# Twenty narrow scans for the rows of nodes in a graph layer, with their limits counted ahead of a branch

## The chip, the cores and the metric

The kernel runs on one core of a Trainium2 chip. The metric is the device time of one launch in microseconds: 3378.7 us is the median of three runs before the change (3378.27 to 3379.26). The profile is one execution on the same core, with a span of 3379.6 us.

## What is computed

One layer of a graph network over 10000 nodes with 512 features and 160000 edges, sorted by destination. The layer adds three things to `x`: a message sum over edges, a linear attention, and a mixture of experts whose weights are set once, from the mean of all rows.

```python
xn = _layernorm(x, axis=-1)
# message sum
h = jnp.matmul(xn, W)
msgs = h[edge_src] * edge_weight[:, None]
agg = jax.ops.segment_sum(msgs, edge_dst, num_segments=X.shape[0])
gnn = jax.nn.relu(agg + bias)
# linear attention, 8 heads of 64
q = jax.nn.softmax(q, axis=-1) * scale
k = jax.nn.softmax(k, axis=-2)
context = jnp.einsum('bhnd,bhne->bhde', k, v)
out = jnp.einsum('bhde,bhnd->bhne', context, q)
# x = x + gnn + gamma_layer_norm(out @ w_out); then x = x + experts(_layernorm(x))
dst = jnp.minimum((10000 * jax.random.uniform(..., (160000,)) ** 2.0).astype(jnp.int32), 9999)
```

The last line matters here. The destinations are 10000 times the square of a uniform number, so about 160000 times the root of node/10000 edges come before those of a node: low nodes have many edges, high ones few.

## The kernel before

**Chunks.** The nodes are worked in twenty chunks of 512 (the last has 272), each as four sub-rows of up to 128 partitions: partition p and sub-row s hold node base + 4p + s.

**Key stage.** For each chunk TensorE turns the normalised rows (`pt`, L197), multiplies them with the key and query weights (`pk`, `pq`, L205), and adds up `ek` times rows (`pc`, L779). ScalarE takes exponentials. VectorE adds the keys' sums (`kacc`, L766), makes the softmax of the queries from PSUM (`qs`, `qt`, L188 to L190), copies turned rows out of PSUM (L199) and adds `pc` to `G` (L782). The program order of TensorE is written out by hand (`manual_schedule`); the other engines' order is made by a scheduler that places each instruction by its inputs and by its estimate of when engines come free.

**Edges.** The 160000 edges are 1250 tiles of 128. GpSimd fetches the 128 source rows of a tile with one indirect transfer (`msg`, L485) into one of 24 slots. Tiles are joined to windows: the first 896 tiles in pairs, the other 354 alone, so there are 802 windows (`NW`; `PAIRED` is 448). `bases` holds the first destination of each window, the same in all partitions. For each tile VectorE builds a selection matrix `sel` (L492, L494) that places an edge's weight in one of 32 rows, row = destination minus the window's base. TensorE multiplies `sel` with `msg` (`pm`, L503), ScalarE copies the sum, and it is stored to `part_d`, 32 rows to a window. A node that two windows share is put right later (`carry`, L557 to L579). In the key stage a planner (`work`) places edge products in TensorE's order, one tile for each 0.93 us of planned work.

**Finding rows.** To add a node's sum, the kernel must know its row in `part_d`. Row = node + sum over all windows whose base is at most the node of `jump`, where `jump` is 32 minus the gap to the base before. `find_rows` (L443) does this for a chunk: four scans over all 802 windows (L449), each a `scalar_tensor_tensor` that compares `bases` with the nodes, multiplies with `jump` and adds up along the row; then two small steps (L454, L455) turn the four sums into row numbers `row_of`. It is called for five chunks when the edges are placed, and for the other fifteen at the end of their own chunk in the key stage; there `behind` keeps the scans after the last `G` addition. The intermediate `past` and the `gap` of `place_edges` share one buffer (tag `past`).

**The branch.** The shortcuts hold only for edges that are spread evenly enough. So `place_edges` counts the conditions that hold in the columns of `count`: two sums over tiles and windows, and one comparison for each of ten limits `AT_HAND` (L439). `oddities` adds the columns (L537), lets TensorE add the partitions (L539), and compares with `ALL_GOOD`, the count when all hold. After the key stage every engine loads the result and branches (L614, L615): if any condition fails, a general path runs. The page's profile is of a run that skips it.

**After the branch.** TensorE turns `G` (needs VectorE), makes the context and then works chunk by chunk on attention (`po`) and on the graph product (`pg`), with edge products in between. GpSimd gathers node sums by `row_of` (`at`, L865) between the `msg` gathers. When all edges are done the expert stage runs, with TensorE alone as its pace.

Of the kernel before, what the change touches and what calls it, by code (L numbers as in the profile page):

```python
# [9 lines left out]
F32 = mybir.dt.float32  # L10
I32 = mybir.dt.int32
AF = mybir.ActivationFunctionType
ALU = mybir.AluOpType
# [3 lines left out]

P = 128
SQ = 32
SUB = 4  # L20
EPS = 1e-5
HEAD = 64
QSCALE = HEAD ** -0.5
PAIRED = 448
GROUP = 4
WIN = P // GROUP
# [6 lines left out]
AT_HAND = [(5, 320), (7, 384), (9, 448), (11, 512), (13, 576), (14, 640), (15, 672), (16, 704), (17, 736), (18, 756)]  # L33
# [13 lines left out]
def gps_layer_kernel(  # L47
# [19 lines left out]
    nc = tc.nc  # L67
    N, D = x.shape
    NET = src.shape[1]
# [10 lines left out]
    chunks = []  # L80
    base = 0
    while base < N:
        rows = min(P, (N - base) // SUB)
        chunks.append((base, rows))
        base += rows * SUB
    assert base == N
    NCH = len(chunks)

    def tokens(t, c):
        b, r = chunks[c]  # L90
        return t[b : b + r * SUB, :].rearrange("(p s) d -> p s d", s=SUB)

# [6 lines left out]
    make_identity(nc, ident)  # L99
    half_neg = const.tile([P, SUB], F32, name="half_neg")  # L100
    nc.gpsimd.memset(half_neg, -0.5)
# [13 lines left out]
    for last in sorted({b - a for a, b in zip(CARRIES, CARRIES[1:])}):  # L115
# [3 lines left out]
                                fill=0.0, base=1 - last, channel_multiplier=1)  # L119
    node = const.tile([P, NCH, SUB], F32, name="node")  # L120
    nc.gpsimd.iota(node, pattern=[[P * SUB, NCH], [1, SUB]], base=0, channel_multiplier=SUB,
                   allow_small_or_imprecise_dtypes=True)
# [19 lines left out]
    NW = NET - PAIRED  # L142
# [9 lines left out]
    def behind(inst, other):  # L152

        tc.add_manual_dep(inst.ins, other.ins.name, mybir.DependencyInfo(
            mybir.DependencyClass.NoSync, mybir.DependencyReason.SCHED_ONLY), reason="order of work")
# [81 lines left out]
    def experts_weights():  # L237
# [12 lines left out]
        for j in range(KB):  # L250
            for g in range(P // SQ):
                nc.gpsimd.dma_start(w1_sb[g * SQ : (g + 1) * SQ, j, :], features(w1)[j, g, :, : NBASE * P])
        nc.gpsimd.dma_start(w2_sb, w2[: NBASE * P, :].rearrange("(f p) d -> p f d", p=P))
# [4 lines left out]
    def features(t):  # L258

        return t.rearrange("(g j e) h -> j g e h", g=P // SQ, j=KB)  # L260

    def rows_in(c):

        r = chunks[c][1]
        xn = io_f["in"].tile([P, SUB, D], F32, name="xn2")
        if r % SQ:
            for j in range(KB):
                for g in range(P // SQ):
                    nc.sync.dma_start(xn[:r, :, j * P + g * SQ : j * P + (g + 1) * SQ],
                                      x1_d[c][:, :, g * P + j * SQ : g * P + (j + 1) * SQ])  # L270
# [64 lines left out]
    with ExitStack() as ph:  # L335
# [6 lines left out]
        ep = edge_ctx.enter_context(tc.tile_pool(name="edge", bufs=1))  # L342
        ew = edge_ctx.enter_context(tc.tile_pool(name="edge_w", bufs=3))
# [42 lines left out]
        on_w = ep.tile([P, NET], F32, name="on_w")  # L386
        bases = ep.tile([P, NW + 1], F32, name="bases")
        jump = ep.tile([P, NW], F32, name="jump")
        count = ep.tile([P, 2 + len(AT_HAND)], F32, name="count")
        n_big = ep.tile([1, 2], F32, name="n_big")  # L390
        usable = ep.tile([P, 1], F32, name="usable")
        n_odd = ep.tile([1, 1], I32, name="n_odd")
# [1 line left out]
        def place_edges():  # L394
            nc.sync.dma_start(src_sb, src)
            nc.sync.dma_start(w_sb, edge_w)
            dst_sb = tmp.tile([P, NET], I32, name="dst_sb", tag="whole")
            nc.sync.dma_start(dst_sb, dst)
            row_sb = tmp.tile([P, NET], I32, name="row_sb")
            nc.sync.dma_start(row_sb, dst[0:1, :].to_broadcast([P, NET]))  # L400

            nc.vector.memset(bases[:, 0:1], 0.0)
            nc.vector.memset(bases[:, NW:], FAR)
            nc.vector.tensor_copy(bases[:, 1:PAIRED],
                                  row_sb[:, 2 : 2 * PAIRED].rearrange("p (w j) -> p w j", j=2)[:, :, 0])
            nc.vector.tensor_copy(bases[:, PAIRED:NW], row_sb[:, 2 * PAIRED :])
            gap = ew.tile([P, NW], F32, name="gap", tag="past", bufs=1)
            nc.vector.tensor_tensor(gap, bases[:, 1:], bases[:, :NW], ALU.subtract)
            nc.vector.tensor_copy(place, dst_sb)

            def by_window_of(t, per_window, o, op):

                nc.vector.tensor_tensor(
                    o[:, : 2 * PAIRED].rearrange("p (w j) -> p w j", j=2),
                    t[:, : 2 * PAIRED].rearrange("p (w j) -> p w j", j=2),
                    per_window[:, :PAIRED, None].to_broadcast([P, PAIRED, 2]), op)
                nc.vector.tensor_tensor(o[:, 2 * PAIRED :], t[:, 2 * PAIRED :], per_window[:, PAIRED:NW], op)

            by_window_of(place, bases, place, ALU.subtract)

            by_window_of(place, gap, on_w, ALU.is_equal)
            nc.vector.tensor_tensor(on_w, on_w, w_sb, ALU.mult)


            nc.vector.memset(jump[:, 0:1], 1.0)
            nc.vector.tensor_scalar(jump[:, 1:], gap[:, : NW - 1], -1.0, float(WIN), op0=ALU.mult, op1=ALU.add)


            good = tmp.tile([P, NET], F32, name="good", tag="whole")
            by_window_of(place, gap, good, ALU.is_le)  # L430
            nc.vector.scalar_tensor_tensor(good, place, 0.0, good, op0=ALU.is_ge, op1=ALU.mult)
            nc.vector.scalar_tensor_tensor(good, place, float(WIN - 1), good, op0=ALU.is_lt, op1=ALU.mult,
                                           accum_out=count[:, 0:1])
            nc.vector.tensor_scalar(good[:, :NW], gap, 0.0, None, op0=ALU.is_ge)
            nc.vector.scalar_tensor_tensor(good[:, : NW - 1], gap[:, : NW - 1], float(WIN), good[:, : NW - 1],
                                           op0=ALU.is_lt, op1=ALU.mult, accum_out=count[:, 1:2])

            for i, (n, w) in enumerate(AT_HAND):
                nc.vector.tensor_scalar(count[:, 2 + i : 3 + i], bases[:, w : w + 1],  # L439
                                        float(chunks[n][0] if n < NCH else N), None, op0=ALU.is_ge)  # L440

        ALL_GOOD = P * (NET + NW - 1 + len(AT_HAND))

        def find_rows(c, other):

            at = ew.tile([P, SUB], F32, name="at")
            for s in range(SUB):
                past = ew.tile([P, NW], F32, name="past", bufs=1)
                scan = nc.vector.scalar_tensor_tensor(  # L449
                    past, bases[:, :NW], node[:, c, s : s + 1], jump,  # L450
                    op0=ALU.is_le, op1=ALU.mult, accum_out=at[:, s : s + 1])
                if other:
                    behind(scan, other)
            nc.vector.tensor_tensor(at, at, node[:, c], ALU.add)  # L454
            nc.vector.tensor_scalar(row_of[:, c], at, float(ZERO_ROW), None, op0=ALU.min)  # L455

# [77 lines left out]
        def oddities():  # L534
# [5 lines left out]
            n = ew.tile([1, 2], F32, name="n", bufs=1)  # L540
            nc.vector.tensor_scalar(n[:, 0:1], pn, -1.0, float(ALL_GOOD), op0=ALU.mult, op1=ALU.add)
            nc.vector.tensor_scalar(n[:, 1:2], n_big[:, 0:1], -1.0, 1.0, op0=ALU.mult, op1=ALU.add)
# [66 lines left out]
        def general_path():  # L609

            with ExitStack() as pb:
                fp = pb.enter_context(tc.tile_pool(name="far", bufs=1))
                kp = pb.enter_context(tc.tile_pool(name="with_max", bufs=1, side="right"))
                any_odd = nc.values_load(n_odd[0:1, 0:1], min_val=0, max_val=ALL_GOOD + 2)  # L614
                with tc.If(any_odd > 0):  # L615
# [128 lines left out]
        for c, (_, r) in enumerate(chunks):  # L744
            if c == EARLY:
                normal_rows(NCH)
                place_edges()
                next_nodes()
                oddities()
                for soon in range(ROWS_SOON):  # L750
                    find_rows(soon, None)
                norm_ctx.close()
                done[1] = -6 * PACE
                pools["m"] = edge_ctx.enter_context(tc.tile_pool(name="edge_m", bufs=24,
                                                                 reuse_waits="tile"))
                nc.sync.dma_start(wv, w_qkv_t[:, 2 * D :].rearrange("(k p) d -> p k d", p=P))
                nc.sync.dma_start(wo, w_out_t.rearrange("(k p) d -> p k d", p=P))
# [156 lines left out]
        for c, (_, r) in enumerate(chunks):  # L914
            ot, at = ot_next, held["at"]
# [22 lines left out]
            if c == NCH - 1:  # L938
# [3 lines left out]
                                           op0=ALU.mult, op1=ALU.mult)  # L942
            if c < NCH - 1:
                for s in range(SUB):
                    nc.vector.scalar_tensor_tensor(xsum[:r], ot[:r, s, :], mv[:r, s, 1:2], xsum[:r],
                                                   op0=ALU.mult, op1=ALU.add)
# [55 lines left out]
    more = wp.tile([1, 1], F32, name="more")  # L1002
# [242 lines left out]
    with tc.If(any_more > 0):  # L1245
# [9 lines left out]
        for c, (_, r) in enumerate(chunks):  # L1255
# [8 lines left out]
            for f in blocks:  # L1264
                m, at = fsz[f], (f - NBASE) * P
# [55 lines left out]
```

## Time and profile before

| stretch, us | what runs | TensorE busy | VectorE busy | GpSimd busy | granted clock |
|---|---|---|---|---|---|
| 0 to 100 | first loads, rows normalised | 72.2 of 100 | 77.1 | 72.3 | 0.95 |
| 100 to 126 | rows of the first chunks, scans | 20.9 of 26 | 26.0 | 20.8 | 0.96 |
| 150 to 178 | scans, `sel` builds | 24.7 of 28 | 27.1 | 12.4 | 0.89 |
| 400 to 600 | key stage with edges | 200 of 200 | 101.3 | 149.9 | 1.00 |
| 1200 to 1985 | attention, graph product, edges | 753.8 of 785 | 515.4 | 555.5 | 0.99 |
| 2500 to 3000 | experts | 499.6 of 500 | 249.5 | 0 | 1.00 |

Busy is the time in which an engine carries out instructions of its own; a wait for another engine is idle time and is put down to the one that ended it. The granted clock is the share of TensorE's full clock [...]. GpSimd's 0.95 us for a gather is the time to issue it; the data land some microseconds later.

### The profile page before, as it was taken

Reading aid. Unit: us, or ns where it says so; the run is one execution under the profiler, and the core shown is the slowest. Engines: PE = TensorE matmul, PEld = TensorE weight load, DVE = VectorE, ACT = ScalarE, POOL = GpSimd, SP = SyncE. Lnnn points to the kernel's source line nnn. Section 1 sums busy time; section 2 is a strip of 40 time slices with the busy share of each in tenths; the row PEclk is TensorE's granted clock in tenths of the full one; section 3 lists DMA queues with packets and bytes.
Section 4 is the critical chain, followed back from the end, with each engine's and each line's share of the span. In section 5 each row is a group of like instructions: output and inputs, shape, how many; then the busy total and the mean of one; then the engine's idle time right before and its main releaser. Section 6 shows DMA issues by size and latency. Waiting matters only on the chain.

```text
span 3379.6 us, 37367 instructions
## 1 busy us (share of the span) xinstructions
PE 3270.7 (97%) x12969; PEld 1923.8 (57%) x12969; DVE 1842.5 (55%) x4771; ACT 797.3 (24%) x1626; POOL 1433.4 (42%) x1472
## 2 busy tenths in 40 slices
PE   6999999999999899999999999999999999999998
PEld 3444444444443333333333347888888888888886
DVE  7844545455545456666766576544554455445543
ACT  4412121212121121122222123222222222222211
POOL 6667777777777777777777420000000000000000
PEclk9999999999999999999999999999999999999999
DMA  9778888888878888999989751121212121212111
GB/s 363 262 231 254 275 258 279 257 272 263 268 241 262 290 291 304 309 329 325 329 313 329 235 163 50 50 63 50 88 50 63 54 84 50 63 60 78 50 39 40
DMA packets 218332, 644.96 MB, mean 191 GB/s; under 512 B 35486, under 2 KB 75422, under 8 KB 193786
## 3 DMA queue, kind: packets, MB, share of 16 engines
q0 software_dynamic: 108208, 354.02, 33.5%
q1 hardware_dynamic: 67656, 168.51, 15.2%
q10 hardware_dynamic: 42266, 119.91, 9.1%
q8 instruction: 106, 1.74, 0.2%
q14 instruction: 96, 0.79, 0.1%
HBM read 485.32 MB, written 157.00 MB: 190 GB/s over the span
## 4 chain that ended last, share of the span: by engine, by line
PE 54%; DMA 9%; issue 1%; DVE 1%; POOL 1%; ACT 0%; POOLq 0%; DVEq 0%; ACTq 0%; SPq 0%
PE px L1103 15%; PE pz L1103 10%; PE py L1103 10%; PE po L205 7%; DMA msg<-xn_d,src_sb 6%; PE pg L205 6%; PE pm L503 3%; PE ph L1103 2%; PE pt L197 1%; DMA z_d<-xt 1%; POOL msg L485 1%; DMA xt<-x_d 1%; DMA at<-part_d,row_of 1%; DMA x_d<-ot 0%; PE pcarry L568 0%
## 5 line engine op out<-in xcount | busy, mean ns | idle before, releaser
L485 POOL DMA_INDIRECT msg<-xn_d,src_sb x1250 | 1226.5, 981 | 424.8 <-issue 236.6
L503 PE MATMUL pm<-msg,sel 128*32 128x512 f32 x2504 | 356.2, 603 | 28.7 <-DMA msg<-xn_d,src_sb 28.6
L492 DVE TENSOR_SCALAR sel<-iota_w,place,w_sb 128x31 f32<-128x31 f32 x1250 | 305.9, 317 | 103.9 <-PE pm L503 103.7
L205 PE MATMUL po<-G,qT 128*128 128x512 f32 (+1 forms) x640 | 292.7, 604 | 8.0 <-DMA qT<-qT_d 8.0
L205 PE MATMUL pg<-wq,aT 128*128 128x512 f32 (+1 forms) x640 | 293.5, 607 | 5.9 <-ACT aT L199 5.9
L779 PE MATMUL pc<-xn,ek 128*128 128x512 f32 (+1 forms) x640 | 288.7, 601 | 3.7 <-DVE qt L190 3.7
L205 PE MATMUL pk<-wk,xnT 128*128 128x512 f32 (+1 forms) x640 | 285.7, 599 | 0.0
L205 PE MATMUL pq<-wq,xnT 128*128 128x512 f32 (+1 forms) x640 | 284.5, 597 | 0.0
L506 ACT COPY part<-pm 128x512 f32<-128x512 f32 x201 | 118.1, 587 | 629.7 <-PE pm L503 604.7
L503 PEld LDWEIGHTS pm<-msg,sel 128*32 128x32 f32 x2504 | 68.3, 109 | 282.2 <-issue 196.9
L205 PEld LDWEIGHTS pg<-wq,aT 128*128 128x128 f32 (+1 forms) x640 | 116.9, 189 | 182.9 <-issue 162.9
L205 PEld LDWEIGHTS po<-G,qT 128*128 128x128 f32 (+1 forms) x640 | 116.0, 189 | 171.0 <-issue 147.5
L205 PEld LDWEIGHTS pk<-wk,xnT 128*128 128x128 f32 (+1 forms) x640 | 118.1, 188 | 164.4 <-issue 153.1
L205 PEld LDWEIGHTS pq<-wq,xnT 128*128 128x128 f32 (+1 forms) x640 | 117.5, 187 | 165.3 <-issue 159.2
L1103 PE MATMUL px<-xnT,w_sb 128*128 128x256 f32 (+1 forms) x800 | 203.8, 377 | 6.4 <-DVE u L1138 6.3
L779 PEld LDWEIGHTS pc<-xn,ek 128*128 128x128 f32 (+1 forms) x640 | 118.7, 192 | 145.8 <-issue 141.7
L1103 PE MATMUL px<-w_sb,hh 128*128 128x256 f32 (+1 forms) x800 | 185.7, 379 | 0.0
L161 DVE BATCH_NORM_STATS2 st<-ot 128x6 f32<-128x512 f32 (+1 forms) x160 | 110.2, 689 | 138.4 <-ACT ot L903 137.5
L1103 PE MATMUL py<-xs,w_sum 128*128 128x256 f32 (+1 forms) x800 | 185.0, 374 | 0.0
L1103 PE MATMUL py<-w_sum,hh 128*128 128x256 f32 (+1 forms) x800 | 179.2, 379 | 0.0
L1103 PEld LDWEIGHTS px<-xnT,w_sb 128*128 128x128 f32 x800 | 150.3, 191 | 28.5 <-DVE u L1138 8.8
L1103 PEld LDWEIGHTS py<-w_sum,hh 128*128 128x128 f32 (+1 forms) x800 | 150.0, 188 | 22.7
(270 smaller groups left out, 4438.5 us busy)
## 6 DMA issues: line engine op xcount, KB each, us to landing
part_d<-part ACTq DMA_DIRECT2D x201, 256.0 KB
msg<-xn_d,src_sb POOLq DMA_INDIRECT x1250
xn<-in_x SPq DMA_DIRECT2D x19, 1024.0 KB
xn_d<-xn ACTq DMA_DIRECT2D x19, 1024.0 KB
qT_d<-qT ACTq DMA_DIRECT2D x19, 1024.0 KB
qT<-qT_d SPq DMA_DIRECT2D x19, 1024.0 KB
xt<-in_x SPq DMA_DIRECT2D x19, 1024.0 KB
x_d<-ot SPq DMA_DIRECT2D x19, 1024.0 KB
```

Of the source, the lines that this page charges most:

```text
L161: nc.vector.bn_stats(st[:r, s, :], t[:r, s, :])
L197: nc.tensor.transpose(pt[:, s * r : (s + 1) * r], t[:r, s, kb * P : (kb + 1) * P], ident[:r, :r])
L205: nc.tensor.matmul(po[:r, :], t[:, kb, s * r : (s + 1) * r], w[:, kb, :], start=kb == 0, stop=kb == KB - 1)
L485: nc.gpsimd.indirect_dma_start(out=m[k], out_offset=None, in_=xn_d, in_offset=bass.IndirectOffsetOnAxis(ap=src_sb[:, t0 + k : t0 + k + 1], ...
L492: nc.vector.tensor_scalar(sel[:, k, 1:], iota_w, place[:, t0 + k : t0 + k + 1], w_sb[:, t0 + k : t0 + k + 1], op0=ALU.is_equal, op1=ALU.mult)
L503: nc.tensor.matmul(pm[h * WIN : (h + 1) * WIN, :], sel[:, k, :], m[k] if k < len(m) else m[0], start=j == 0, stop=j == batch - 1, skip_gro ...
L506: nc.scalar.copy(part, pm)
L779: nc.tensor.matmul(pc, ek[:r, s, cb * P : (cb + 1) * P], xn[:r, s, :], start=s == 0, stop=s == SUB - 1)
L1103: nc.tensor.matmul(o, lhs[j], rhs[j], start=start and j == 0, stop=stop and j == n - 1, skip_group_check=True)
```

## The change

The destinations' distribution is known, so the windows that can hold a chunk's nodes are too: `window_at` turns a node into a tile number, 1250 times the root of node/10000, and that into a window. `span(c)` gives a range `lo` to `hi` for a chunk, ten tiles (`SPARE`) wider on both sides. The scans then run over windows lo + 1 to hi - 1 alone. What all windows up to `lo` would have added is known without a scan: their `jump` telescopes to 1 + 32 lo - bases[lo]. One more small instruction adds it.

That a range holds depends on the edges at hand, so each range is checked: base `lo` must be at most the chunk's first node, base `hi` at least its end. These forty comparisons go into forty more columns of `count`, and `ALL_GOOD` grows by as much; if one fails, the general path runs as for the other conditions. `gap` gets a buffer of its own.

```diff
+SPARE = 10
...
-        count = ep.tile([P, 2 + len(AT_HAND)], F32, name="count")
+        count = ep.tile([P, 2 + len(AT_HAND) + 2 * NCH], F32, name="count")
...
-            gap = ew.tile([P, NW], F32, name="gap", tag="past", bufs=1)
+            gap = ew.tile([P, NW], F32, name="gap", bufs=1)
...
-
-        ALL_GOOD = P * (NET + NW - 1 + len(AT_HAND))
+            spans_hold()
+
+        ALL_GOOD = P * (NET + NW - 1 + len(AT_HAND) + 2 * NCH)
+        WIDEST = 256
+
+        def window_at(node, more):
+            tile_no = NET * (node / N) ** 0.5 + more
+            return min(max(int(tile_no / 2 if tile_no < 2 * PAIRED else tile_no - PAIRED), 0), NW)
+
+        def span(c):
+            return window_at(chunks[c][0], -SPARE), window_at(chunks[c][0] + SUB * chunks[c][1], SPARE)
+
+        def spans_hold():
+            for c, (b, r) in enumerate(chunks):
+                for i, w, op, edge in ((0, span(c)[0], ALU.is_le, b), (1, span(c)[1], ALU.is_ge, b + SUB * r)):
+                    at = 2 + len(AT_HAND) + 2 * c + i
+                    nc.vector.tensor_scalar(count[:, at : at + 1], bases[:, w : w + 1], float(edge), None, op0=op)
 
         def find_rows(c, other):
 
             at = ew.tile([P, SUB], F32, name="at")
+            lo, hi = span(c)
             for s in range(SUB):
-                past = ew.tile([P, NW], F32, name="past", bufs=1)
+                past = ew.tile([P, WIDEST], F32, name="past_c", bufs=1)[:, : hi - lo - 1]
                 scan = nc.vector.scalar_tensor_tensor(
-                    past, bases[:, :NW], node[:, c, s : s + 1], jump,
+                    past, bases[:, lo + 1 : hi], node[:, c, s : s + 1], jump[:, lo + 1 : hi],
                     op0=ALU.is_le, op1=ALU.mult, accum_out=at[:, s : s + 1])
                 if other:
                     behind(scan, other)
+
+            nc.vector.tensor_scalar(at, at, bases[:, lo : lo + 1], float(1 + lo * WIN), op0=ALU.subtract, op1=ALU.add)
             nc.vector.tensor_tensor(at, at, node[:, c], ALU.add)
```

## The prediction

> **What bounds the kernel now.** First the page's busy times and slices.
>
> ```profile
> PE 3270.7 (97%) x12969; PEld 1923.8 (57%) x12969; DVE 1842.5 (55%) x4771; ACT 797.3 (24%) x1626; POOL 1433.4 (42%) x1472
> PE   6999999999999899999999999999999999999998
> ```
>
> TensorE is busy for 3270.7 of 3379.6 us. All its idle time is 109 us, so an edit of VectorE work is worth only what it takes out of these 109 us, or off whatever else sets the pace in some stretch. Next the groups, for the price of what the change shrinks.
>
> ```profile
> L449 DVE SCALAR_TENSOR_TENSOR past<-bases,node,jump 128x802 f32<-128x802 f32 x80 | 85.0, 1062 | 1.0
> L449 DVE DVE_READ_ACCUMULATOR past<-bases,node,jump 128x1 f32 x80 | 6.5, 82 | 0.0
> ```
>
> Eighty scans of 802 elements, 85.0 us in all: 2.5% of the span, but on an engine that is 55% busy. So the timeline of TensorE must tell where a scan stands before it. Its only idle time between 40 and 1138 us is here (start, length, and in brackets the idle time before it and who ended it):
>
> ```profile
> 116.68 1.47 PE L197 MATMUL pt<-ident,xn 128*128 128x128 f32 x12
> 120.01 0.63 PE L197 MATMUL pt<-ident,xn 128*128 128x128 f32 x4 [1.86 <-DVE minus L366]
> 123.85 8.80 PE L779 MATMUL pc<-xn,ek 128*128 128x512 f32 x16 [3.21 <-DVE qt L190]
> 134.24 7.03 PE L779 MATMUL pc<-xn,ek 128*128 128x512 f32 x16
> ...
> 168.57 1.04 PE L197 MATMUL pt<-ident,xn 128*128 128x128 f32 x8
> 172.00 1.08 PE L197 MATMUL pt<-ident,xn 128*128 128x128 f32 x4 [2.39 <-DVE qt L190]
> 173.56 1.08 PE L197 MATMUL pt<-ident,xn 128*128 128x128 f32 x4 [0.48 <-DVE qt L190]
> 175.12 8.83 PE L779 MATMUL pc<-xn,ek 128*128 128x512 f32 x16 [0.48 <-DVE qt L190]
> ```
>
> Two stalls, both on the softmax rows of L190: VectorE is behind. Around the first it is busy 26.0 of 26 us (100 to 126), around the second 27.1 of 28 (150 to 178). Thirteen of the first twenty scans lie from 88 to 121 us, three from 134 to 142, four from 153 to 159.
>
> A third wait stands at the branch:
>
> ```profile
> 1146.14 3.64 PE L197 MATMUL pt<-ident,G 128*128 128x128 f32 x16 [7.23 <-DVEq L615]
> ```
>
> Last, GpSimd. Its gathers (L485) start every 1.25 us, 0.95 busy and 0.30 between. Up to 985 us some wait for TensorE to free a message slot (8.03 us at 208, 2.07 at 911, 3.08 at 985). After that, to 1903 us, they go back to back with few gaps: 634 gathers and 72 more of L865, 706 x 1.25 = 883 us of a stretch of 914. From 985 on the gathers set the pace. And there some take longer:
>
> ```profile
> 1030.73 0.95 POOL L485 DMA_INDIRECT msg<-xn_d,src_sb  x1 [0.30 <-issue]
> 1031.98 1.74 POOL L485 DMA_INDIRECT msg<-xn_d,src_sb  x1 [0.30 <-DMA msg<-xn_d,src_sb]
> ```
>
> and VectorE's timeline at that place:
>
> ```profile
> 1031.84 1.06 DVE L449 SCALAR_TENSOR_TENSOR past<-bases,node,jump 128x802 f32<-128x802 f32 x1
> ```
>
> The gather that began 0.14 us after a scan took 1.74 us and ended just after it (1033.72, with an add of L766 behind the scan) where its neighbour took 0.95.
>
> [...] sixteen matmuls took 8.80 and 8.83 us after the two stalls, 7.03 elsewhere, and the granted clock from 150 to 178 us was 0.89. [...]
>
> **The change, part by part.**
>
> (1) Shorter scans. From the generated `dst`, the twenty ranges hold 145, 68, 53, 47, 43 windows in the first five chunks and 27 to 60 in the rest, 1066 in place of 16040. Every comparison of a limit holds for them, so the branch stays untaken. [...]
>
> (2) Added: 40 comparisons into `count`, and one `tensor_scalar` for each chunk. Their like are L439 (three in 0.26 us, a step of 0.065) and L455 (0.07). 40 x 0.065 = 2.6 us and 20 x 0.07 = 1.4 us. Bounds for the comparisons: 0.065 as a step, 0.14 as a whole duration (L439's median), so 2.6 to 5.6 us; I take 2.6, since they don't depend on each other.
>
> (3) The order. The scheduler doesn't leave the freed time empty. In the built order the twenty scans of the first five chunks, the comparisons and 22 to 27 `sel` builds (L492; 6 before) now come ahead of the first stall's softmax rows. I added up the VectorE steps from the timeline of before over both orders. Up to the two rows that end the first stall's waits (L190 at 119.18 and 123.03) the sum moves by -0.5 and +0.1 us: the first stall stays. Up to the rows of the next chunk it is 12.4 us less: the `sel` builds that filled 156 to 170 us are done by then. VectorE idled 8.57 us at 141.7 and takes part of them there. So the second stall goes.
>
> What it is worth: from the start of its transposes (168.57) to the next `pc` took 6.55 us, in the undisturbed place (132.49 to 134.24) 1.75; that `pc` took 8.66 in step, undisturbed 6.95. So 4.8 + 1.7 = 6.5 us. TensorE then reaches the first edge product (207.1) 6.5 us earlier. Its messages were gathered from 169.9 to 200.4, and GpSimd waited 8.03 us for that product; 1.5 us of that wait remain. So the gathers, which up to 985 us wait for TensorE, move along, and with them the gather-paced stretch and all that follows.
>
> (4) The three last scan groups (at 1028, 1084 and 1136 us) lie where gathers set the pace. Their four hit gathers took 1.08, 1.74, 1.69 and 1.71 against 0.95: 2.4 us. [...] I take 2.2 us. The scan groups before 985 us also lengthen gathers, by about as much each, but there GpSimd waits for TensorE anyway: nothing.
>
> (5) The branch. VectorE reached it at 1141.6, after the four scans of the last chunk; now `ksum` (TensorE's 1138.9) is last, and it arrives at about 1139.3. TensorE restarts some 2.3 us earlier. But four fewer gathers are queued before the branch (738, not 742), the drain gap at 1150.75 stays, and after it TensorE waits for messages (1161.6). Between 0 and 2.3; alone it gives nothing, since gathers set the pace; with (4) it keeps TensorE out of their way. I take 0.
>
> The 60 scans after 200 us cost TensorE nothing: it is busy 100% from 220 to 1000 us. Nothing after the branch is touched.
>
> Sum: 6.5 + 2.2 = 8.7 us. 3378.7 - 8.7 = 3370.0.
>
> **Rivals.** (a) The gathers, not TensorE, hold the line from their start: xn_d's last write frees them at 169.9, whatever TensorE does. Then the 6.5 us are swallowed and (4) remains: 3376.5. For it: 1326 gathers x 1.25 = 1658 us of 1734. Against it: GpSimd's 39.3 us of waits for `pm` from 180 to 1140.
> (b) The first stall shrinks too, because the small steps are cheaper than I price them. The whole stall is 7.17 - 1.75 + 1.7 = 7.1 us: 3362.9. For it: 13 scans lie there. Against it: the sums over the order.
> (c) Nothing carries: the waits just move to the next DMA. 3378.7. For it: the message waits after 1160.
> (d) Slower: the four gathers put behind the branch meet the weight and row loads that start there (one gather at 1152.12 took 9.46 us to land) and cost their 4 x 1.25 = 5.0 us, while (a) eats the early gain: 3378.7 - 2.2 + 5.0 = 3381.5. The comparisons at 0.14 would add up to 3 us to the first stall.
>
> **How the numbers follow.** Forecast 0.63, (a) 0.13, (b) 0.10, (c) 0.07, (d) 0.07. The forecast's own spread is 3367 to 3372.5 (1 us of drain or branch each way, 2.8 for the comparisons' upper bound, which is partly hidden). The range takes in most of (a) and the near half of (b): 3365 to 3376.6. 0.2% is 6.8 us, 3371.9: faster holds (b) and nine tenths of the forecast, 0.66; same (a), (c) and the rest, 0.27; slower 0.07.
>
> **What would show it.** The scan's group at about 0.2 to 0.3 us mean. The wait of `pt` on `qt` near 172 gone and `pc` at 7.0; the waits near 118 to 124 still there. The first `pm` near 200.6, GpSimd's wait before it 1.5 us. Gathers near 1030, 1088 and 1138 at 0.95 to 1.2. The span to the last gather 8 to 9 us shorter, the last stage as long as before. Wrong if GpSimd shows new waits after the branch, or if the first stall moves by more than 1 us.

## The result, and the profile after

The changed kernel's median was 3365.1 us over four runs, beside 3379.0 for the kernel before: ratio 0.9959, 95% interval 0.9942 to 0.9976, so 8 to 20 us off. Nineteen more runs of the changed kernel, beside 51 of the kernel before, narrow this to 0.9975 (0.9968 to 0.9982): 8.4 us off, between 6.1 and 10.8, median 3369.7. The forecast was 8.7 off, 3370.0. The first four runs had fallen on the good side; how far runs differ is part of what follows.

First the page of the changed kernel, its busy times:

```profile
PE 3262.2 (97%) x12969; PEld 1926.0 (57%) x12969; DVE 1790.6 (53%) x4831; ACT 796.8 (24%) x1626; POOL 1413.5 (42%) x1472
```

VectorE lost 51.9 us, GpSimd 19.9. Then VectorE's groups, the scan, the read of its sum, the extra step and the forty comparisons (count, then busy time and mean ns):

```profile
L467 DVE SCALAR_TENSOR_TENSOR past_c<-bases,node,jump 128x53 f32<-128x53 f32 (+18 forms) x80 | 22.3, 278 | 1.6
L467 DVE DVE_READ_ACCUMULATOR past_c<-bases,node,jump 128x1 f32 x80 | 6.6, 82 | 0.0
L473 DVE TENSOR_SCALAR at<-at,bases 128x4 f32<-128x4 f32 x20 | 4.9, 246 | 0.5
L459 DVE TENSOR_SCALAR count<-bases 128x1 f32<-128x1 f32 x40 | 2.9, 137 | 0.0
```

A scan takes 278 ns in the mean, not 1062. TensorE's timeline at the two stalls and at the branch:

```profile
116.30 1.04 PE L198 MATMUL pt<-ident,xn 128*128 128x128 f32 x8
117.91 0.63 PE L198 MATMUL pt<-ident,xn 128*128 128x128 f32 x4 [0.58 <-DVE qt L191]
120.17 1.09 PE L198 MATMUL pt<-ident,xn 128*128 128x128 f32 x4 [1.63 <-DVE minus L367]
124.47 9.86 PE L799 MATMUL pc<-xn,ek 128*128 128x512 f32 x16 [3.21 <-DVE qt L191]
...
170.25 1.91 PE L198 MATMUL pt<-ident,xn 128*128 128x128 f32 x16
171.99 7.03 PE L799 MATMUL pc<-xn,ek 128*128 128x512 f32 x16
...
202.16 1.92 PE L523 MATMUL pm<-msg,sel 128*32 128x512 f32 x16
...
1138.30 3.65 PE L198 MATMUL pt<-ident,G 128*128 128x128 f32 x16 [4.31 <-DVEq L635]
```

The second stall is gone: sixteen transposes without a wait, `pc` at 7.03. The first one stayed and cost more: `pc` started at 124.47 (before 123.85) and took 9.86 (8.80). The first edge product came at 202.16 instead of 207.08, TensorE's restart after the branch at 1138.30 instead of 1146.14.

How far TensorE is ahead of the kernel before (its lead), in the two profiles of the changed kernel (start of the same product in each trace, subtracted):

| at (time in before) | 116 us | 169 | 187 | 1110 | 1147 | 1200 | 1500 | 1900 | 1930 | end |
|---|---|---|---|---|---|---|---|---|---|---|
| changed | 0.4 | -1.7 | 4.9 | 4.9 | 7.8 | 5.9 | 8.8 | 7.1 | 17.0 | 17.2 |
| changed, again | 1.0 | -0.8 | 5.8 | 5.8 | 8.2 | 7.4 | 6.8 | 8.6 | 8.5 | 8.1 |

Up to the branch the two agree within 1 us. The 9 us between them arise between 1900 and 1930, at the last messages, which the kernel before waited for:

```profile
1912.57 1.88 PE L503 MATMUL pm<-msg,sel 128*32 128x512 f32 x2 [5.03 <-DMA msg<-xn_d,src_sb]
1915.45 1.93 PE L503 MATMUL pm<-msg,sel 128*32 128x512 f32 x6 [0.99 <-DMA msg<-xn_d,src_sb]
1917.31 8.15 PE L205 MATMUL pg<-wq,aT 128*128 128x512 f32 x16
```

and the changed kernel, again, too:

```profile
1904.65 1.88 PE L523 MATMUL pm<-msg,sel 128*32 128x512 f32 x2 [5.68 <-DMA msg<-xn_d,src_sb]
1907.27 1.93 PE L523 MATMUL pm<-msg,sel 128*32 128x512 f32 x6 [0.73 <-DMA msg<-xn_d,src_sb]
1909.13 7.86 PE L206 MATMUL pg<-wq,aT 128*128 128x512 f32 x16
```

In the first profile of the changed kernel no wait stood there, and the sixteen products after it took 7.13 us. Over all profiles on chips of this speed the wait was 0 to 10.7 us, in no relation to the edit: none in the changed kernel and two others, 10.7 with narrow scans in the last three chunks. So it is a landing that differs from run to run, for a cause that no run shows.

### The profile page after: what moved, and what is told of

Its sections match the earlier page's. It is cut to its first block, busy times and chain, and to the rows that moved or that the text cites. A ratio compares the mean times of both kernels' runs of the same rounds, so it can differ in the third digit from the quotient of the medians.

```text
span 3362.2 us, 37437 instructions
## 1 busy us (share of the span) xinstructions
PE 3262.2 (97%) x12969; PEld 1926.0 (57%) x12969; DVE 1790.6 (53%) x4831; ACT 796.8 (24%) x1626; POOL 1413.5 (42%) x1472
## 3 DMA queue, kind: packets, MB, share of 16 engines
q8 instruction: 106, 1.74, 0.2%
## 5 line engine op out<-in xcount | busy, mean ns | idle before, releaser
L505 POOL DMA_INDIRECT msg<-xn_d,src_sb x1250 | 1212.3, 970 | 426.5 <-issue 230.2
L1123 PEld LDWEIGHTS px<-w_sb,hh 128*128 128x128 f32 (+1 forms) x800 | 151.0, 189 | 22.6
```

The source lines that it names most:

```text
L505: nc.gpsimd.indirect_dma_start(out=m[k], out_offset=None, in_=xn_d, in_offset=bass.IndirectOffsetOnAxis(ap=src_sb[:, t0 + k : t0 + k + 1], ...
L1123: nc.tensor.matmul(o, lhs[j], rhs[j], start=start and j == 0, stop=stop and j == n - 1, skip_group_check=True)
```

## The experiments

Time differences are the ratio and its interval times the time of the kernel before, run beside each kernel. It took 3378 us on the two chips of the usual speed. Four kernels ran on a third, slower Trainium2 chip ("the other chip", 3662 us), described at the end. "6.4 off" means 6.4 us faster than the kernel before; in brackets stands the 95% interval.

**Count only.** The kernel before with the forty comparisons, scans as they were.

```diff
+            spans_hold()
...
-        ALL_GOOD = P * (NET + NW - 1 + len(AT_HAND))
+        ALL_GOOD = P * (NET + NW - 1 + len(AT_HAND) + 2 * NCH)
```

> The kernel before with its full scans, and the forty comparisons added. My theory (VectorE is the bound from 100 to 126 us, and forty steps of 0.065 us come ahead of the first stall's softmax rows, but the scheduler then puts two fewer scans and two fewer sel builds there): the first stall changes by less than 1 us and the time stays at 3379, within 2 us. Rival 1 (the comparisons are what made the first stall grow by 1.9 us in the changed kernel): 3381 to 3382. Rival 2 (they cost more than their step because each waits for the one before): 3384 or more.

Measured: 1.0 us off (4.1 off to 2.0 more). Within its noise the added count costs nothing. In its trace TensorE fell 2.3 us back at the first stall and stayed 1.8 behind up to the branch, more than the 1 us of my theory; the interval holds that too. Nineteen comparisons in a row took 1.23 us in the changed kernel's trace, 0.061 from each start to the next. That they wait for one another (rival 2) is out, and so by its time is rival 1 (3 us more).

**No count.** The changed kernel without the forty comparisons.

```diff
-            spans_hold()
```

> The changed kernel with the forty comparisons left out, so that nothing guards the ranges. My theory: the scheduler fills their place with 13 more sel builds ahead of the same softmax rows (13 x 0.21 = 2.7 us against 40 x 0.065 = 2.6), so the first stall stays as long and the time stays at 3365, within 1.5 us. Rival (the comparisons are what made the first stall longer): 1.9 to 2.6 us off, 3362.5 to 3363.

Measured: 11.1 off the kernel before (6.8 to 15.2), median 3369.6, where the changed kernel's nineteen runs have 3369.7. The first stall did not shrink: its three waits are 1.25, 1.63 and 3.32 us, 6.2 in sum, beside 5.4 in the changed kernel. In VectorE's order 38 instructions that build `sel` now come ahead of the chunk's second softmax row, not 25: the scheduler filled the place, as expected. The intervals don't exclude a gain of 2 us; the trace shows none.

**First five and last fifteen.** Narrow scans for one group of chunks alone, with the comparisons of these (shown against the changed kernel).

```diff
+            narrow = c < ROWS_SOON
...
-                    past, bases[:, lo + 1 : hi], node[:, c, s : s + 1], jump[:, lo + 1 : hi],
+                    past, bases[:, lo + 1 : hi] if narrow else bases[:, :NW], node[:, c, s : s + 1],
+                    jump[:, lo + 1 : hi] if narrow else jump,
```

The other has `c >= ROWS_SOON`.

> Narrow scans (with their ten comparisons) for the first five chunks alone, full scans for the other fifteen. The forecast's steps: the second stall goes, 6.5 us; the first stall's growth of 1.9 us as in the changed kernel takes some back; 3374 to 3374.5 (4.6 to 5 off). Rival 1 (the 5 us that the changed kernel gained beyond the forecast in the gather stage come from starting it earlier): 3368 to 3370. Rival 2 (a late wait swallows the early gain, and the gain is in the late scans): 3377 to 3379.

> Full scans for the first five chunks, narrow scans (with their thirty comparisons) for the other fifteen. The forecast's steps: both early stalls stay, 2.2 us of longer gathers go: 3376.5. Rival 1 (the branch reached 2.3 us earlier counts too, as the trace's 2.9 us between 1028 and 1146 us suggests, and the late waits for messages go with it): 3371 to 3374. Rival 2 (nothing carries without the early gain): 3378.5 to 3379.5.

Measured: first five 6.4 off (3.7 to 9.5), last fifteen 7.8 off (3.0 to 12.5). The first agrees with the forecast's early part: second stall gone, TensorE 6.0 ahead at 187 us, and at the branch no more than that (5.5), since the last scans were full. Its interval takes in part of rival 1 as well. The second was too much for 2.2 and fits its rival 1, and its trace had a surprise. VectorE in it, where the last chunk's rows are awaited, and then TensorE at the place of the second stall:

```profile
142.35 0.69 DVE L162 BATCH_NORM_STATS2 st<-xn 68x6 f32<-68x512 f32 x1 [1.17 <-DMA xn<-in_x]
```

```profile
168.69 1.91 PE L198 MATMUL pt<-ident,xn 128*128 128x128 f32 x16
170.44 7.03 PE L804 MATMUL pc<-xn,ek 128*128 128x512 f32 x16
```

No second stall, though the twenty scans ahead of these rows were full! The difference is in the first line: the load of the last chunk's rows landed at 142.35. In the kernel before it was awaited for 8.57 us:

```profile
150.26 0.69 DVE L161 BATCH_NORM_STATS2 st<-xn 68x6 f32<-68x512 f32 x1 [8.57 <-DMA xn<-in_x]
```

In the trace VectorE ran nothing else in these 8.57 us: the scans and `sel` builds queued behind the statistics stood still with them. So a new theory: the second stall needs both, a late load and long scans. The next experiments were to part them.

**More loads under way.** The kernel before with full scans and one more buffer for the rows that are loaded and normalised.

```diff
-        a_io = norm_ctx.enter_context(tc.tile_pool(name="a_io", bufs=4))
+        a_io = norm_ctx.enter_context(tc.tile_pool(name="a_io", bufs=5))
...
-            part = ew.tile([P, D], F32, name="part")
+            part = ew.tile([P, D], F32, name="part", bufs=2)
```

> The kernel before with five instead of four buffers for the rows that are loaded and normalised (and two instead of three for the edge sums, for the room). Theory (the second stall comes from VectorE standing idle for 8.57 us for the last chunk's load, with the scans and sel builds queued behind it): the load lands earlier, the idle time shrinks and the second stall goes though the scans are full; 5 to 6.5 us off, 3372 to 3373. Rival (the amount of scan work makes the second stall, whatever the load does): 3377 to 3379.

Measured (other chip): 9.9 off (4.0 to 15.7). VectorE's and TensorE's lines at the place:

```profile
138.18 0.69 DVE L161 BATCH_NORM_STATS2 st<-xn 68x6 f32<-68x512 f32 x1 [2.76 <-DMA xn<-in_x]
```

```profile
168.59 1.91 PE L197 MATMUL pt<-ident,xn 128*128 128x128 f32 x16
170.34 7.03 PE L779 MATMUL pc<-xn,ek 128*128 128x512 f32 x16
```

The second stall is gone, with not one scan made shorter. The edit moved more than this one load, though: TensorE's transposes at the first stall began 5.1 us later than in the kernel before and made it up by 150 us. The cleaner case, one program with a late and with an early landing, comes with the last three below.

**Held, full.** The kernel before, its first twenty scans and six groups of `sel` builds held behind the second chunk's last softmax row.

```diff
+                if i < 6:
+                    behind(one, held["after"])
...
-                    find_rows(soon, None)
+                    find_rows(soon, held["after"])
...
-                softmax_rows(qt, r, s, pq)
+                last_row = softmax_rows(qt, r, s, pq)
+            if c == EARLY - 2:
+                held["after"] = last_row
```

> The kernel before with full scans, only held in the same way: the first twenty scans and six groups of sel builds behind the second chunk's last softmax row. Theory (the amount of work counts): the first stall goes, but twenty scans of 0.98 us and 54 sel builds of 0.21, 31 us, now lie ahead of the third chunk's softmax rows and lengthen the second stall by as much as the first one gave; 3376 to 3381. Rival (the place alone matters, VectorE's idle time at 142 us takes the scans): both stalls shrink, 3368 to 3372.

Measured (other chip): 3.3 slower (1.5 faster to 8.1 slower). The last load was early here too (144.24), and yet:

```profile
167.99 0.63 PE L197 MATMUL pt<-ident,xn 128*128 128x128 f32 x4 [0.42 <-DVE qt L190]
171.80 0.63 PE L197 MATMUL pt<-ident,xn 128*128 128x128 f32 x4 [3.19 <-DVE at L454]
172.74 8.80 PE L783 MATMUL pc<-xn,ek 128*128 128x512 f32 x16 [0.32 <-issue]
```

With all the scans crowded ahead of these rows the stall came back, as the theory said; that both stalls shrink is out. The amount counts, and so does the room that the load leaves.

**Held.** The same edit of the changed kernel, first on the other chip, then on a usual one; then with the fifth load buffer.

> The changed kernel with the first twenty scans and the first six groups of sel builds held behind the second chunk's last softmax row on VectorE. My theory: both stalls go, but in the changed kernel GpSimd hardly waits for TensorE before the first edge product any more, so the first stall's 7 to 9 us are not carried, the gathers start from xn_d's last write as before; 0 to 3 us off the changed kernel, 3363 to 3367, beside a before of 3378.1. Rival (the gathers start earlier too, since the statistics of the last rows come earlier on VectorE, so TensorE's gain is carried): 5 to 9 us off it, 3357 to 3361.

> The changed kernel with the first scans and sel builds held behind the second chunk's last softmax row, again, where TensorE has no waits for issue. Where it ran before, TensorE was 3.4 us ahead of the changed kernel's 4.9 at 187 us (8.3 against the kernel before) and the first gather started at 167.0, not 172.3. Theory (the gathers' start carries it): 3 to 5 us faster than the changed kernel beside it. Rival (nothing is carried beyond the changed kernel's gain): within 1.5 us of it.

> The same with five buffers for the rows that are loaded (two for the edge sums). Theory (VectorE stands idle for loads at 111, 118 and 143 us in the held kernel, and an earlier load takes these waits away): 2 to 4 us faster than the held kernel, the best of all, 8 or more off the changed kernel. Rival (xn_d's last write, paced by the transfers, sets the start of the gathers whatever VectorE does): as the held kernel, within 1.5 us.

Measured: held 9.5 off the kernel before (4.4 to 14.3) on the other chip, 11.5 off (7.1 to 15.5) on a usual one; with five buffers 10.5 off (7.4 to 13.2). All are faster than the kernel before. Against the changed kernel, run beside them, held is 3.2 us faster in the mean of nine runs (0.0 to 6.1, by drawing anew from the single times many times over), with five buffers 0.5 (1.6 slower to 2.5 faster). So held is the best of all by its figures, at the edge of the noise against the changed kernel. The fifth buffer did not bring the 2 to 4 us expected of it: beside held it was 2.8 us slower in the mean (0.4 faster to 5.7 slower). TensorE in held, where the first stall was, up to the first edge product:

```profile
116.04 1.91 PE L198 MATMUL pt<-ident,xn 128*128 128x128 f32 x16
121.51 8.80 PE L803 MATMUL pc<-xn,ek 128*128 128x512 f32 x16 [3.56 <-DVE qt L191]
...
166.23 1.91 PE L198 MATMUL pt<-ident,xn 128*128 128x128 f32 x16
167.98 7.03 PE L803 MATMUL pc<-xn,ek 128*128 128x512 f32 x16
...
198.15 1.92 PE L525 MATMUL pm<-msg,sel 128*32 128x512 f32 x16
```

and GpSimd's first gathers there:

```profile
166.35 1.26 POOL L505 DMA_INDIRECT msg<-xn_d,src_sb  x1 [14.03 <-DMA xn_d<-xn]
...
199.47 1.02 POOL L505 DMA_INDIRECT msg<-xn_d,src_sb  x1 [3.03 <-PE pm L525]
```

The gathers began 4.4 us earlier than in the changed kernel beside it (170.76), since the last write of `xn_d` came 4.4 us earlier. My first theory, that nothing of it is carried, had left this out. Two things brought it. The last rows' statistics come at 143.04 instead of 151.53. That alone isn't enough: in held with five buffers they came at 139.07, and the first gather at 169.31. The rest is TensorE, as ScalarE shows in held:

```profile
156.13 0.66 ACT L794 ACTIVATE pq<-pq,usable 128x512 f32<-128x512 f32 x1 [1.53 <-PE pq L206]
...
157.51 0.50 ACTq L375 DMA_DIRECT2D xn_d<-xn  x1
```

ScalarE issues the last write right behind an exponential that waits for TensorE's `pq`. So once the statistics are early, the write follows TensorE: in six profiles with statistics before 147 us the first gather starts 0.08 to 0.12 us after TensorE's transposes near 168 us. Held has these at 166.23, since TensorE lost less time up to there, last fifteen at 168.69, where the statistics came at 142.35. With a first gather 0.1 us after them, at 168.8 in last fifteen, some 2 of the 4.4 us are the statistics' and 2.5 TensorE's, an estimate.

What remains of the first stall, 3.56 us, lies behind VectorE's waits for loads (5.81 us before 105.25, 1.07 before 110.55, 1.98 before 118.03). With a fifth buffer these waits moved (2.26 at 112.46, 4.39 at 122.71) instead of going, and TensorE was back at 169.21, the first gather at 169.31.

**Last three.** Narrow scans for the three chunks that lie in the gather-paced stretch, on the other chip and on a usual one (`narrow = c >= NCH - 3`).

> Narrow scans (with their six comparisons) for the last three chunks alone, full scans for the other seventeen. The forecast's step (4): four gathers no longer lengthened, 2.2 us off the 3378.1 of before, 3376. With step (5) at what the traces show between 1110 and 1140 us (about 3 us for both steps): 3375. Rival (the late narrow scans also take away waits of the gather stage, which the run with fifteen narrow chunks leaves possible): 6 us or more off, 3372 or less. Rival 2 (nothing of it is carried to the end): 3378.

> Narrow scans for the last three chunks alone, again, where TensorE has no waits for issue. The forecast's steps (4) and (5): 2.2 to 3 us off the kernel before, ratio 0.9991 to 0.9994. Rival (late narrow scans also take away waits of the gather stage): 6 us or more off, 0.9982 or less.

Measured: 8.8 off (1.5 to 16.1) on the other chip, 4.4 off (1.0 to 8.1) on a usual one. The forecast's 2.2 to 3 lies in both, 6 too; the time doesn't part them. In the trace TensorE gained 2.8 us between 1110 and 1147 us, as in the changed kernel (2.9 and 2.4), in the one without comparisons (3.1) and with the last fifteen narrow (3.1); with the first five alone it lost 0.5. But the profile also has 6 us that this edit can't have brought: its last load landed at 146.54, and the second stall was absent once more, with the first scans full. On the other chip the same program, with VectorE's instructions in the same order up to there, had the load at 151.83 and the stall. So with full scans the landing decides, not the program. The chip doesn't: on either kind a late landing came with the stall (150.26, 151.83), an early one without (146.54, 138.18). Why the last fifteen gave 7.8 and not 3 isn't settled: an early landing as in its profile, in most of its seven runs, would do it, and so would chance.

**Changed, again.** The changed kernel, untouched.

> The changed kernel again, beside many runs of the kernel before, to separate what it gains from what one run and the next differ by. My theory (the part beyond the forecast's 8.7 us lies in landings that differ from run to run; the second stall comes and goes in the kernel before with the landing of the last rows' load): 9 to 12 us off, ratio 0.9965 to 0.9973. Rival (all of the 13.9 us is systematic): 13 us or more off, 0.9962 or less.

Measured: 8.4 off (6.1 to 10.8), just below the 9 to 12 of my theory, which the interval reaches; the rival's 13 is out.

**The other chip.** On it the kernel before took 3662.4 us (67 runs), 8% more. Its traces follow the others up to some 165 us. From the first gathers on TensorE stands with nothing that the profile shows as a cause. The longest of TensorE's waits in held there (us in total, times, longest):

```profile
PE pm L525 <- issue: 50.7, 45, 5.5
PE pt L198 <- issue: 34.1, 35, 1.8
...
PE po L206 <- issue: 20.7, 17, 9.5
```

In sum 153 to 172 us of such waits stand in the four traces from there, and none in those from the usual chips: over half of the 284 us that this chip is slower. So these four are used for what they show before the gathers start, and for the ratio to the kernel before on the same chip.

## Why the prediction was right

The size was right: 8.7 us forecast, 8.4 (6.1 to 10.8) measured with enough runs. By its own steps:

**(1) and (2), the sizes.** VectorE's busy time fell by 51.9 us. The trace of before gives an estimate: from its start to that of the next instruction a scan of 802 elements took 0.98 us (101.89 to 102.87), and the 96 elements of L572 took 0.23 (170.71 to 170.94), so 1.06 ns for an element and 0.13 us besides. Then 80 x 0.98 = 78 us less 80 x 0.13 + 4264 x 0.00106 = 15 is 63 us off, less 4 for what is added. It counts steps from start to start, which is not quite the same measure as busy time. A scan of 68 windows and the `sel` build behind it went by in 0.42 us, 0.21 each, where the estimate has 0.20 for the scan. The comparisons' step of 0.065 held (0.061).

**(3), the first stall stays.** It did, but TensorE lost 2.1 and 1.8 us between 116 and 169 us in the two profiles of the changed kernel, 2.6 without the comparisons, where I had -0.5 to +0.1. That the edit caused this isn't shown: with full first scans TensorE lost there too, 2.3 us with the count only and 1.3 and 1.7 with the last three narrow, while the last fifteen gained 0.3. The one profile of the kernel before may just have a short first stall. The sum over VectorE's order was nearly right: TensorE's waits there are 5.4 us (0.58, 1.63, 3.21) and 5.8 in the second profile, before 5.1. What I missed is the clock: `pc` took 9.86 and 9.62 us after them, not 8.80. Over the 9.86 the granted clock was 0.72, over the 8.80 it was 0.81, and over the next `pc` of before, 7.03 us long, 1.00. In the kernel before it was 0.99 from 122 to 124 us, 0.50 from 124 to 126 and 1.00 again from 128; in the changed kernel it was 0.50 from 120 to 130 us, so already ahead of the longest wait. That wait was 3.21 us in both. Behind two waits of 2.40 and 2.75 us, in last three, `pc` took 9.88. The price of this stall was therefore not its wait alone, and 1 us of it changed with the same longest wait; what sets the clock is not shown. The comparisons didn't do it: without them the stall was no shorter.

**(3), the second stall goes.** It went in every profile with narrow first scans, and TensorE gained 6.6 us between 169 and 187 us, forecast 6.5. But I took the stall of the kernel before as a fixed thing. It is not:

| kernel | first twenty scans | last rows' statistics begin, us | TensorE's waits in the second stall, us |
|---|---|---|---|
| before | full | 150.26 | 3.35 |
| count only | full | 149.13 | 3.16 |
| last three, other chip | full | 151.83 | 3.22 |
| last three | full | 146.54 | 0 |
| last fifteen | full | 142.35 | 0 |
| more loads, other chip | full | 138.18 | 0 |
| held, full, other chip | full, held | 144.24 | 3.93 |
| changed; again | narrow | 153.12; 151.53 | 0 |
| no count; first five | narrow | 153.26; 151.49 | 0 |
| held; held, other chip | narrow, held | 143.04; 143.06 | 0 |
| held, five buffers | narrow, held | 139.07 | 0 |

With full scans in their own order the stall is there from 149.13 on and not up to 146.54; narrow scans bear a landing at 153. I had seen VectorE's 8.57 us of idle time and used it as room for `sel` builds, without asking what ended it, and whether it would be there in the next run. The two lines of last three show it best: one program, once with the stall and once without. How often the kernel before has the stall can't be said from one profile of each kernel. Where it is absent, narrow scans can gain nothing there, so the 6.5 us are what a run gains that has the stall. The mean of first five, 6.4 off (3.7 to 9.5), agrees in size.

**(3), it is carried.** Yes: TensorE's lead of 4.9 and 5.8 us at 187 stands unchanged at 1110 us. GpSimd's wait before the first `pm`, 8.03 us before, fell to 0.84 and 1.80, with 1.5 forecast. That agreement is part chance: the forecast had a lead of 6.5 us and a start of the gathers that doesn't move; the lead was 4.9 and 5.8, and the gathers began 2.4 and 0.9 us later. But GpSimd still waited for TensorE there, and not the other way round, against rivals (a) and (c).

**(4), the gathers under the late scans.** From the start of message gather 627 to that of 743 took 148.95 us before, 146.78 and 146.52 after: 2.2 and 2.4, forecast 2.2. Summed over this stretch, what the gathers took beyond 0.95 us each fell from 2.6 to 0.4 and 1.0 us; the rest of the 2.4 is gaps between them. With the first five alone narrow, two gathers there took 1.73 us again. From 200 us to the branch, all gathers of before that began 0.13 to 0.19 us after the start of a full scan took 1.69 to 1.74 us; one that began 0.36 after it took 1.52, those at 0.61 took 1.26, one at 0.80 took 1.08. Those that began ahead of a scan, up to 0.08 us after its start or from 0.96 on took 0.94 to 0.97. In the changed kernel's first profile no gather beside a narrow scan took over 0.97, though eight began 0.11 to 0.24 us after the start of one. The longest of the stretch, 1.39 at 1088.64, stands beside an addition to `kacc` (L786). So in these traces a full scan lengthened the gathers that began some 0.1 to 0.8 us into it, a narrow one lengthened none; by what means no run shows. The forecast's 2.2 is the 2.4 of the four hit gathers less 0.2 allowed for narrow scans, the author's estimate. But that gathers alone set the pace from 985 us on isn't so in every run: with the last three narrow and in held with five buffers the gathers were as short (0.2 and 0.4 us beyond 0.95), yet the stretch took 148.70 and 148.95 us, as one wait of 3.05 and 3.15 us for TensorE's `pm` at 1082 took the gain back.

**(5), the branch, taken as 0.** TensorE's lead grew by 2.9 and 2.4 us from 1110 us to its restart behind the branch, somewhat more than the 2.3 worked out. That it was worth nothing, as taken, fits what follows: behind the branch GpSimd stood more (its gap at 1150.75 was 1.04 us before, the one at 1149.43 was 1.55 in the changed kernel; over message gathers 743 to 776 its gaps beyond 0.30 us were 3.8 and 3.6 us in sum, before 1.7; in the second profile the two largest, 1.86 and 1.51 us, ended with TensorE). Gather 777 began at 1193.5 in both profiles, 1200.4 before: 6.9 earlier for (3), (4) and (5) together, where the forecast had 8.7.

**The rest.** After 1200 us the trace wanders by several microseconds either way between two profiles of one program; forecast and result agree there only in the mean. Since the steps that can be followed give 6.9 us and not 8.7, that the mean came to 8.4 is in part luck. In the one of the first four runs that was profiled the wait for the last messages was missing, about 6 us; for the other three the excess stays unexplained. The slower rival (d) fell: the gathers behind the branch cost 2 us of gaps, not 5 and more.

The prediction named two signs of being wrong, and both came: the first stall moved by more than 1 us, and GpSimd had new waits after the branch. In its main part the mechanism stood: the second stall goes, and the gain is carried to the branch. Around it two terms taken as nothing were some 2 us each in these traces, the first of them perhaps not from the edit.

## What to carry to other kernels

Before a stall is priced, ask what else has to happen for it: here a load that lands between 138 and 153 us decides whether full scans stall TensorE at the second place, and with shorter scans no landing up to 153 us did. Work that nobody waits for (here scans whose rows are read 1000 us later, and the first selection matrices) belongs behind the work that another engine waits for; holding it there is a small edit, and gave another 3.2 us in the mean (0.0 to 6.1). And four runs were too few for 0.2%: they gave 13.9 us where nineteen gave 8.4.

## What the runs showed of the hardware

Single executions of one program on one chip spread over 13 us (3360.9 to 3374.0 for the changed kernel); the wait for the last messages alone was 0 in one of its profiles and 6.4 us in the other, and up to 10.7 over all kernels. Another chip ran the kernel before in 3662 us; the four traces from that chip have 153 to 172 us of TensorE waits that no engine or transfer in the profile explains, all after the indirect gathers begin. What was queued on VectorE behind a wait for a transfer stood still with it: the statistics of 68 rows held back scans, `sel` builds and softmax rows for 8.57 us before and for 10.62 without the comparisons. Sixteen products of `pc` took 7.03 us at a granted clock of 1.00, 8.80 at 0.81 and 9.86 at 0.72. A gather's issue on GpSimd took 0.95 us in the median, before up to 1.74 beside a scan of 802 windows up to the branch, and in the changed kernel at most 0.97 beside scans of 27 to 60 and up to 1.44 beside an addition to `kacc`. After the branch, where no scan runs, one of before took 2.42 (1352.70, beside L909 and L932). The data came later: before, a `pm` that waited for the gather issued at 1152.12 started at 1161.62, 9.50 us on.
